# Corner sums through PSUM slots, an inverse transform moved into another loop, and new due times for a hand-made instruction order

## The chip, the core and the metric

The kernel runs on one core of a Trainium2 chip. The metric is device time in microseconds (us) of one execution over the whole batch of four samples. An engine is called by its short name: PE is the matmul engine (PEld its weight loads), DVE the vector engine, ACT the scalar engine, POOL the GpSimd engine and SP the engine that issues plain DMAs.

## What is computed

The input is x of shape (4, 96, 128, 128). Four layers follow one another, each as x + layer(groupnorm(x)):

```python
x = x + L0(gn(x))   # 1x1 projection and 3x3 depthwise conv, a selective scan over 16384 pixels in both directions, 1x1 projection
x = x + L1(gn(x))   # 3x3 conv of 32 channels, fractional and plain Fourier mixing of 64, then a 3x3 conv of all 96
x = x + L2(gn(x))   # deformable 3x3 conv
x = x + L3(gn(x))   # mask, 2-D cosine transform, four state-space scans on quadrants, inverse cosine transform
```

Layer 2 is where the change begins. Small convolutions give for each output pixel and each of nine taps an offset and a mask; the tap's sample is a bilinear mix of four corners, times the mask, and the nine samples of 96 channels go through one weight matrix each:

```python
for k in range(9):
    py, px = base_y + i + dy[k], base_x + j + dx[k]
    samp = ((1-wy)*(1-wx)*v00 + (1-wy)*wx*v01 + wy*(1-wx)*v10 + wy*wx*v11) * mask[k]
    out += einsum('bchw,oc->bohw', samp, weight[:, :, i, j])
```

## The kernel before, in words

**Two lanes and a scan.** The samples are pipelined. `front` (layers 0 and 1, and the offsets of layer 2) of sample b+1 is lane 1; `back` of sample b (layer 2's gather, the head of layer 3, and its forward cosine transform) is lane 0. Both are issued together, and after them `layer3` runs the scans of sample b alone. The inverse transform of sample b-1 (`inverse`) stands at the head of lane 1. So the execution is: front of sample 0 alone; M0 (back 0, front 1) and a scan stage; M1 (back 1, inverse 0, front 2) and a scan stage; M2 (back 2, inverse 1, front 3) and a scan stage; M3 (back 3, inverse 2) and a scan stage; the last inverse alone. M0 to M3 are names that this text uses for the merged stages.

**How the order is made.** Nothing in a lane goes to the engines directly. `Program.record` (line 296) keeps each operation with its data dependencies and an estimated cost (`Program.cost`, line 351). `Program.issue` (line 372) then plays the stage through: it takes the operation that can start soonest, and among those of its engine that could start within `LATENCY` = 0.2 us of that moment the one with the smallest key. The order so found is the program order of each engine; the engines then run it at their own pace, each in order, and wait on semaphores. An operation's key is its due time: each lane is first played alone (`measure`), and the key is the start found there, divided by the last start of its lane, so that both lanes go from 0 to 1 together. Before the change, inverse and front are measured one after the other as one lane; where a stage has no inverse, its front begins at the inverse's end in that list. A scalar-engine operation that needs another function table is taken to start 1.3 us later. `weigh`, `turn` and `finish` are recorded at fixed places of the gather's loop, but their place in the queues comes from this planner.

**The gather (`gather`, line 1270).** For each of 128 image rows, nine indirect DMAs on POOL (one a tap) fetch, for 128 pixels, the four corners of 96 channels each from a table in DRAM into `l_g`, a tile of 128 partitions x 9 taps x 384 numbers; three rows can be held. `weigh` (line 1297) makes the sums of corners in two halves, five taps and four. In each half, ACT multiplies corner 0 of every tap by its weight (one number a partition) into `l_acc`, a PSUM tile of 5 x 96 numbers, of which there is one; DVE then adds corner 1 of every tap onto it in place, then corner 2 in place, and then corner 3 into the SBUF tile `l_sm`. `turn` transposes `l_sm` on PE and ACT copies the transposes to `l_sT` (one copy for the first half, two for the second). `finish` multiplies four rows at a time with the weights, and DVE adds bias and the residual.

**Layer 0 (`layer0`, line 601).** Statistics of the input; then pool `l0a`, the convolution: per group of 512 pixels nine matmuls and one for the gate, two silus on ACT, two stores; then pool `l0b`, the scan: 64 pieces of 512 pixels, each with a softplus in several ACT operations, DVE products and a DVE scan. Its PSUM pool has five banks under the tags a (2), b (1) and c (2); c is used in the scan alone.

**The inverse (`inverse`, line 1461).** 24 pieces of four channels: load, four matmuls (`t_p`), copy by ACT (`t_t`), four matmuls, DVE adds the residual, store; in PSUM banks of its own, two for each of the two products.

Of the kernel before, what the change touches and what calls it, by code (L numbers as in the profile page):

```python
# [9 lines left out]

# [226 lines left out]
class Program:  # L237
# [6 lines left out]
    SPAN = (1.0, 1.0)  # L244
    ENGINES = {"tensor": "PE", "vector": "DVE", "scalar": "ACT", "gpsimd": "POOL", "sync": "SP"}
    TABLES = {AF.Silu: 1, AF.Exp: 2, AF.Ln: 2, AF.Sqrt: 3, AF.Sigmoid: 4, AF.Sin: 5}

    def __init__(self, tc, engines):
# [4 lines left out]
        self.count, self.starts = [0, 0], ([], [])  # L253
# [22 lines left out]
    def measure(self, lane, steps):  # L276
        self.trial, self.lane = True, lane
        tried = []
        self.tried = tried
        run(steps)  # L280
        self.issue(lane)
        at = self.starts[lane]
        t0 = at[-1] + 1e-3 if at else 0.0
        at += [t0 + op.start for op in tried]
        self.end()
        self.trial = False

    def end(self):
        self.issue(0)
        self.issue(1)  # L290
        for pool in self.kept:
            pool.close()
        self.kept, self.count = [], [0, 0]
        self.restart()

    def record(self, engine, name, args, kw):
# [6 lines left out]
            key=self.count[self.lane], wait=0, ready=0.0, then=[], done=False, table=None,  # L303
        )
        if self.trial:
            self.tried.append(op)
        else:
            at = self.starts[self.lane]
            op.key = self.SPAN[self.lane] * at[self.count[self.lane]] / at[-1]
        self.count[self.lane] += 1  # L310
# [40 lines left out]
    def cost(self, engine, name, out, ins):  # L351
# [9 lines left out]
        if engine == "ACT":  # L361
            return 0.12 + (0.0009 if name == "copy" else 0.0011) * n, None
# [7 lines left out]
        return (0.1 if n < 200 else 0.14) + n / (1900 if fast else 960), None  # L370

    def issue(self, lane):

        while self.left[lane]:
            starts = []
            for op in self.able:
                start = max(self.free[op.engine], op.ready)
                if op.table and self.table and op.table != self.table:
                    start += 1.3
                starts.append((start, op.key, op.lane, len(starts), op))  # L380
# [5 lines left out]
            self.able.remove(op)  # L386
            engine, name, args, kw = op.call
# [102 lines left out]
NB = H // BR  # L490
# [3 lines left out]
class Net:  # L494
# [99 lines left out]
    def front(self, xin, T):  # L594

        T.x1, T.x2 = self.plane("x1"), self.plane("x2")
        yield from self.layer0(xin, T)
# [3 lines left out]
    def layer0(self, xin, T):  # L601
# [3 lines left out]
        with self.program.pool(name="l0w", bufs=1) as wp, self.program.pool(name="l0p", bufs=1, space=PSUM) as ps:  # L605
# [44 lines left out]
            with self.program.pool(name="l0a", bufs=3) as wa:  # L650
# [24 lines left out]
                yield from staggered((block(i) for i in range(NB)), 16)  # L675

            with self.program.pool(name="l0b", bufs=3) as wb:
# [96 lines left out]
    def layer1(self, T):  # L774
        nc, a = self.nc, self.a
        mix_d = [self.plane(f"mix{i}", (4, 32, L)) for i in range(2)]
# [493 lines left out]
    def gather(self, T, wp, wb, ps):  # L1270
# [25 lines left out]

        def weigh(row, m):
# [4 lines left out]
            acc = ps.tile([128, 5, C], F32, name="l2_acc", tag="acc", bufs=1)  # L1302
            w4 = work[row // 4].w4
            taps = range(5 * m, 5 + 4 * m)
            for q in range(4):
                for k in taps:
                    at = 36 * (row % 4) + 4 * k + q
                    g, w = gts[row][:, k, q * C : (q + 1) * C], w4[:, at : at + 1]
                    a_ = acc[:, k - 5 * m, :]
                    if q == 0:  # L1310
                        nc.scalar.activation(a_, g, AF.Copy, scale=w)
                    else:
                        o = sms[row][:, k, :] if q == 3 else a_
                        nc.vector.scalar_tensor_tensor(o, g, w, a_, ALU.mult, ALU.add)
# [103 lines left out]
    def transform2(self, src, mat, ps, wt, tags, extra, done):  # L1418
# [4 lines left out]
        def piece(cb):  # L1423
# [7 lines left out]
            p1 = ps.tile([128, 4, 128], F32, name="t2_p1", tag=tags[2])  # L1431
# [6 lines left out]
            p2 = ps.tile([128, 4, 128], F32, name="t2_p2", tag=tags[3])  # L1438
# [22 lines left out]
    def inverse(self, T, out):  # L1461

        nc = self.nc
        if self.program.trial:
            T.yd_d, T.x3 = self.plane("yd_d"), self.plane("x3")
# [727 lines left out]
```

## Time and profile before

| what | us |
|---|---|
| median of 3 runs (18076.4 to 18091.04) | 18077.28 |
| the profiled execution, its own time | 18104.76 |
| span of the profiled execution, first to last instruction | 18103.0 |
| busy in the span: PE / DVE / ACT / POOL | 14334.4 / 13403.8 / 9535.0 / 10677.0 |
| gathers on POOL, 4608, mean of one | 4498.8, 0.976 |
| DVE products into l_acc, 9216, mean of one | 2964.5, 0.322 |
| DVE products into l_sm, 4608, mean of one | 1141.3, 0.308 |
| ACT products into l_acc, 4608, mean of one | 1582.8, 0.344 |

A profile page of this kernel gives all operations the same line, 65, since a recorder issues them; groups are told apart by tile names, output before the arrow and inputs after it. Where the busy time of a group is below its count times the mean, its instructions overlap one another. The page's busy shares are means over stages with different limits, so the reading goes by stretches of time. The boundaries of the stages are seen from the tiles that belong to each: the first front runs from 0 to 1621 us, M0 to 4073, M1 from 5812 to 8340, M2 from 10077 to 12607, M3 from 14345 to 16290, the last inverse from 18028 to the end, with the scan stages between.

### The profile page before, as it was taken

Reading aid. Unit: us, or ns where it says so; the run is one execution under the profiler, and the core shown is the slowest. Engines: PE = TensorE matmul, PEld = TensorE weight load, DVE = VectorE, ACT = ScalarE, POOL = GpSimd, SP = SyncE. Lnnn points to the kernel's source line nnn. Section 1 sums busy time; section 2 is a strip of 40 time slices with the busy share of each in tenths; the row PEclk is TensorE's granted clock in tenths of the full one; section 3 lists DMA queues with packets and bytes.
Section 4 is the critical chain, followed back from the end, with each engine's and each line's share of the span. In section 5 each row is a group of like instructions: output and inputs, shape, how many; then the busy total and the mean of one; then the engine's idle time right before and its main releaser. Section 6 shows DMA issues by size and latency. Waiting matters only on the chain. (4 is left out here: it accounts for less than half of the span.)

```text
span 18103.0 us, 171591 instructions
## 1 busy us (share of the span) xinstructions
PE 14334.4 (79%) x41152; PEld 6500.9 (36%) x41152; DVE 13403.8 (74%) x26226; ACT 9535.0 (53%) x20127; POOL 10677.0 (59%) x9556
## 2 busy tenths in 40 slices
PE   7896887988898787898999687798899722248898
PEld 2263323543333332634333332454333311123334
DVE  1625696678998587577999678566999766668997
ACT  1612463337776364335777356334777522227776
POOL 0102664527888565443888666451888766647887
PEclk9998887999999887898999788798999855579999
DMA  3525666550001657553000556665000254440001
GB/s 81 161 78 168 180 175 201 172 182 14 8 8 51 190 173 207 155 177 99 8 8 8 158 175 180 186 185 163 6 9 8 84 148 142 142 125 13 8 7 49
DMA packets 1189539, 1940.84 MB, mean 107 GB/s; under 512 B 191984, under 2 KB 711600, under 8 KB 1169456
## 3 DMA queue, kind: packets, MB, share of 16 engines
q1 hardware_dynamic: 893616, 1023.60, 19.4%
q0 software_dynamic: 294912, 906.26, 17.1%
q8 instruction: 329, 5.39, 0.1%
q14 instruction: 682, 5.59, 0.1%
HBM read 1473.67 MB, written 455.61 MB: 107 GB/s over the span
## 5 line engine op out<-in xcount | busy, mean ns | idle before, releaser
L65 POOL DMA_INDIRECT l_g<-quad_d,l_i x4608 | 4498.8, 976 | 4204.9 <-ACT l_acc L65 1827.8
L65 POOL TENSOR_TENSOR l_hc<-l_h,l_cs 128x512 f32<-128x512 f32 x3072 | 3854.1, 1274 | 846.6 <-PE l_py L65 267.5
L65 DVE SCALAR_TENSOR_TENSOR l_acc<-l_g,l_v,l_acc 128x96 f32<-128x96 f32 x9216 | 2964.5, 322 | 1816.8 <-ACT l_acc L65 1540.5
L65 DVE TENSOR_TENSOR_SCAN l_h<-l_dA,l_carry,l_dB 128x512 f32<-128x512 f32 x3072 | 3916.3, 1275 | 166.0 <-ACT l_carry L65 72.9
L65 ACT ACTIVATE l_acc<-l_g,l_v 128x96 f32<-128x96 f32 x4608 | 1582.8, 344 | 3396.8 <-DVE l_sm L65 2755.2
L65 ACT ACTIVATE l_dA<-l_dl,l_al 128x512 f32<-128x512 f32 x3072 | 2182.7, 722 | 803.4 <-DVE l_h L65 802.7
L65 PE MATMUL l_pt<-ident,l_sm 128*128 128x128 f32 (+1 forms) x3584 | 843.5, 343 | 2037.8 <-DVE l_sm L65 1954.8
L65 PE MATMUL l_py<-l_hc,ident 128*128 128x512 f32 x4608 | 2385.9, 607 | 20.2 <-POOL l_hc L65 12.1
L65 DVE TENSOR_TENSOR l_dB<-l_du,l_pB 128x512 f32<-128x512 f32 x3072 | 2135.1, 695 | 319.1 <-POOL l_du L65 28.1
L65 PE MATMUL l_pB<-l_bc,pick 128*128 128x512 f32 x3072 | 1769.3, 576 | 567.1 <-DVE l_dB L65 535.3
L65 ACT COPY l_cs<-l_pC 128x512 f32<-128x512 f32 x3072 | 1783.0, 580 | 629.6 <-PE l_pC L65 533.5
L65 PE MATMUL l_pC<-l_bc,pick 128*128 128x512 f32 x3072 | 1543.7, 503 | 112.5 <-ACT l_cs L65 102.1
L65 PEld LDWEIGHTS l_pt<-ident,l_sm 128*128 128x128 f32 (+1 forms) x3584 | 536.5, 157 | 2774.3 <-issue 2096.9
L65 PEld LDWEIGHTS l_pB<-l_bc,pick 128*128 128x128 f32 x3072 | 580.8, 189 | 2228.5 <-DVE l_dB L65 2132.1
L65 DVE SCALAR_TENSOR_TENSOR l_sm<-l_g,l_v,l_acc 128x96 f32<-128x96 f32 x4608 | 1141.3, 308 | 132.0 <-PE l_pt L65 88.7
L65 PE MATMUL l_pu<-l_xq,l_wc 96*64 96x512 f32 (+1 forms) x2048 | 1074.4, 614 | 13.6 <-ACT l_xq L65 13.6
L65 PE MATMUL l_pc<-rows,l_wc 96*96 96x508 f32 (+2 forms) x2304 | 1065.8, 605 | 14.0 <-DVE rows L65 14.0
L65 PE MATMUL l_p<-rows,l_c 96*96 96x508 f32 (+2 forms) x2304 | 1044.2, 597 | 24.6 <-DMA rows<-cat_d 21.8
L65 PEld LDWEIGHTS l_py<-l_hc,ident 128*128 128x128 f32 x4608 | 877.2, 192 | 379.5 <-issue 174.3
L65 POOL TENSOR_TENSOR l_hc<-l_hc 128x512 f32<-128x512 f32 x768 | 977.6, 1273 | 55.2
L65 PE MATMUL l_pc<-l_sT,l_wk 128*96 128x512 f32 (+1 forms) x1792 | 1002.9, 676 | 1.2 <-ACT l_sT L65 1.2
L65 PEld LDWEIGHTS l_pC<-l_bc,pick 128*128 128x128 f32 x3072 | 582.7, 190 | 995.5 <-ACT l_cs L65 670.6
(252 smaller groups left out, 20676.5 us busy)
## 6 DMA issues: line engine op xcount, KB each, us to landing
quad_d<-l_qt SPq DMA_DIRECT2D x124, 768.0 KB
x<-l_x SPq DMA_DIRECT2D x384, 192.0 KB
l_g<-quad_d,l_i POOLq DMA_INDIRECT x4608, 3.4
mix<-l_mx SPq DMA_DIRECT2D x256, 256.0 KB
sp_in<-mix SPq DMA_DIRECT2D x256, 256.0 KB
l_uc<-u_d SPq DMA_DIRECT2D x256, 192.0 KB
l_x<-x SPq DMA_DIRECT2D x256, 192.0 KB
l_xs<-x SPq DMA_DIRECT2D x116, 256.0 KB
```

The source lines that it names most:

```text
L65: ins = op(*args, **kw).ins
```

## The change

Three things are changed, and the planner's numbers with them. First, `weigh` makes two ACT products a tap (corners 0 and 2) into slots of one PSUM tile of five slots that is kept for the whole gather and used in turn; DVE adds corner 1 onto the first and corner 3 onto the second, writing to SBUF (`l_sm` and a new tile `l_part`), and one DVE addition a half row joins the two. Second, `inverse` no longer stands ahead of the front but is handed to `layer0`, where it is taken in turn with the blocks of the convolution; its matmuls use layer 0's two PSUM banks of tag c, which then serve both products. Where there is no front (M3 and the end), it runs alone as before, on two banks instead of four. Third, due times are kept by plan (front, back, both, inverse) and each plan is divided by its own last start; during layer 0's scan the due times advance at a tenth of the pace, from there to the beginning of layer 1. The costs of short ACT and DVE operations are raised, and a table switch now costs its 1.3 us only in the time that is played, while in the choice it adds 0.006 to the key.

```diff
     SPAN = (1.0, 1.0)
+    SWITCH = 0.006
...
+    def go(self, lane, plan):
+        self.lane, self.at, self.count = lane, {**self.at, lane: self.starts[plan]}, 0
+
+    def measure(self, lane, plan, steps):
+        self.trial, self.lane, self.tried, self.count = True, lane, [], 0
         run(steps)
-        self.issue(lane)
-        at = self.starts[lane]
-        t0 = at[-1] + 1e-3 if at else 0.0
-        at += [t0 + op.start for op in tried]
         self.end()
-        self.trial = False
+        now = before = 0.0
+        for op in sorted(self.tried, key=lambda op: op.start):
+            now += op.pace * (op.start - before)
+            op.due, before = now, op.start
+        self.starts[plan] = [op.due for op in self.tried]
+        self.trial, self.pace = False, 1.0
...
-            return 0.12 + (0.0009 if name == "copy" else 0.0011) * n, None
+            return (0.12 if n > 200 else 0.25) + (0.0009 if name == "copy" else 0.0011) * n, None
...
-        return (0.1 if n < 200 else 0.14) + n / (1900 if fast else 960), None
+        return (0.125 if n < 200 else 0.14) + n / (1900 if fast else 960), None
+
+    def switches(self, op):
+        return bool(op.table and self.table and op.table != self.table)
...
-                if op.table and self.table and op.table != self.table:
-                    start += 1.3
-                starts.append((start, op.key, op.lane, len(starts), op))
+                late = self.SWITCH * self.switches(op)
+                starts.append((start, op.key + late, op.lane, len(starts), op))
...
+            if self.switches(op):
+                start += 1.3
...
-            with self.program.pool(name="l0a", bufs=3) as wa:
+            with self.program.pool(name="l0a", bufs=3) as wa, self.program.pool("l3i", 2) as wt:
...
-                yield from staggered((block(i) for i in range(NB)), 16)
-
+                jobs = [staggered((block(i) for i in range(NB)), 16)]
+                yield from staggered(jobs + ([beside(ps, wt)] if beside else []), 1)
+
+
+            self.program.pace = 0.1
             with self.program.pool(name="l0b", bufs=3) as wb:
...
     def layer1(self, T):
         nc, a = self.nc, self.a
+        self.program.pace = 1.0
...
+        acc = ps.tile([128, 5, C], F32, name="l2_acc", tag="acc", bufs=1)
+        turns = itertools.count()
+
         def weigh(row, m):
...
-            acc = ps.tile([128, 5, C], F32, name="l2_acc", tag="acc", bufs=1)
-            w4 = work[row // 4].w4
-            taps = range(5 * m, 5 + 4 * m)
-            for q in range(4):
-                for k in taps:
-                    at = 36 * (row % 4) + 4 * k + q
-                    g, w = gts[row][:, k, q * C : (q + 1) * C], w4[:, at : at + 1]
-                    a_ = acc[:, k - 5 * m, :]
-                    if q == 0:
-                        nc.scalar.activation(a_, g, AF.Copy, scale=w)
-                    else:
-                        o = sms[row][:, k, :] if q == 3 else a_
-                        nc.vector.scalar_tensor_tensor(o, g, w, a_, ALU.mult, ALU.add)
+            taps = slice(5 * m, 5 + 4 * m)
+            part = wb.tile([128, 5, C], F32, name="l2_part", tag="part")
+            sm = sms[row][:, taps]
+            g4 = gts[row][:, taps].rearrange("p k (q c) -> p k q c", c=C)
+            for k in range(5 - m):
+                at = 36 * (row % 4) + 4 * (5 * m + k)
+                w = [work[row // 4].w4[:, at + q : at + q + 1] for q in range(4)]
+                for q, out in ((0, sm), (2, part)):
+                    slot = acc[:, next(turns) % 5, :]
+                    nc.scalar.activation(slot, g4[:, k, q, :], AF.Copy, scale=w[q])
+                    nc.vector.scalar_tensor_tensor(
+                        out[:, k, :], g4[:, k, q + 1, :], w[q + 1], slot, ALU.mult, ALU.add
+                    )
+            nc.vector.tensor_tensor(sm, sm, part[:, : 5 - m], ALU.add)
...
-            p1 = ps.tile([128, 4, 128], F32, name="t2_p1", tag=tags[2])
+            p1 = ps.tile([128, 4, 128], F32, name="t2_p1", tag=tags[2], bufs=2)
...
-            p2 = ps.tile([128, 4, 128], F32, name="t2_p2", tag=tags[3])
+            p2 = ps.tile([128, 4, 128], F32, name="t2_p2", tag=tags[3], bufs=2)
...
-            tags = ("in", 4), ("mid", 2), "a", "b"
-            yield from self.transform2(T.yd_d, dct, ps, wt, tags, take, put_out)
+        tags = ("in", 4), ("mid", 2), "c", "c"
+        yield from self.transform2(T.yd_d, dct, ps, wt, tags, take, put_out)
+
+    def inverse_alone(self, T, out):
+        with self.program.pool("l3ip", 2, PSUM) as ps, self.program.pool("l3i", 2) as wt:
+            yield from self.inverse(T, out, ps, wt)
...
+        if b + 1 == n and b > 0 or b == n:
+            program.go(1, "inverse")
+            run(net.inverse_alone(samples[b - 1], o_all[b - 1]))
+        elif b > 0:
+            program.go(1, "both")
+            run(net.front(x_all[b + 1], samples[b + 1], inverse(samples[b - 1], o_all[b - 1])))
+        elif b + 1 < n:
+            program.go(1, "front")
             run(net.front(x_all[b + 1], samples[b + 1]))
```

## The prediction

> **What bounds the kernel now.** I read the busy shares by stretch first, with stretches cut where the stages begin and end. Columns: stretch, length, busy us (count) of PE, PEld, DVE, ACT, POOL, granted clock, DMA share, GB/s.
>
> ```profile
> 0.00:1621.00 1621.00, 1367.92 (x4314) 659.80 (x4314) 651.58 (x1120) 527.87 (x1103) 83.63 (x68) 0.95 0.40 114
> 1621.00:4073.00 2452.00, 2007.84 (x6176) 944.61 (x6176) 1763.87 (x4796) 1073.53 (x2737) 1263.03 (x1248) 0.87 0.62 183
> 4073.00:5812.00 1739.00, 1536.45 (x3728) 622.62 (x3728) 1553.47 (x1736) 1294.06 (x2272) 1418.50 (x1140) 0.97 0.03 9
> 5812.00:8340.00 2528.00, 2045.23 (x6560) 1000.98 (x6560) 1781.46 (x4820) 1090.34 (x2761) 1261.98 (x1248) 0.87 0.63 186
> 14345.00:16290.00 1945.00, 674.20 (x2246) 361.69 (x2246) 1195.33 (x3707) 565.47 (x1653) 1134.55 (x1184) 0.62 0.51 148
> ```
>
> In order: front of sample 0 alone; M0 (back of sample 0 beside front of 1); a layer-3 scan stage, which four times makes 6952 us and is not edited; M1 (M2 is its twin at 2530); M3 (back of 3 beside the third inverse). No engine fills M0 to M3, so their phases come next: convolution, layer-0 scan and layer 1 alone in the first front, then the same three in M1.
>
> ```profile
> 118.00:397.00 279.00, 275.04 (x640) 105.22 (x640) 12.03 (x11) 42.04 (x65) 0.00 (x0) 1.00 0.27 74
> 397.00:746.00 349.00, 316.50 (x704) 111.82 (x704) 301.38 (x384) 295.43 (x546) 83.43 (x64) 0.97 0.43 127
> 746.00:1427.00 681.00, 626.66 (x2368) 363.49 (x2368) 179.98 (x325) 109.12 (x285) 0.00 (x0) 0.93 0.38 110
> ...
> 6057.00:6395.00 338.00, 321.72 (x850) 130.84 (x850) 183.31 (x581) 119.46 (x307) 177.72 (x183) 0.97 0.58 171
> 6395.00:6992.00 597.00, 477.34 (x1040) 173.54 (x1040) 536.11 (x1237) 410.78 (x927) 381.84 (x344) 0.85 0.60 174
> 6992.00:8028.00 1036.00, 864.01 (x3007) 460.31 (x3007) 674.80 (x2029) 349.61 (x1024) 517.62 (x540) 0.87 0.62 182
> ```
>
> The same stretches for the gather's tile alone count 183, 280 and 540 gathers, at nine a row: 20, 31 and 60 rows. The scan is bound by DVE (536 of 597); a row costs it (597-349)/31 = 8.0 us. The convolution is bound by PE (322 of 338).
>
> What bounds the gather itself is seen in M3, where it is nearly alone (timeline: start, length, instructions merged, idle time before and who ended it):
>
> ```profile
> 15003.72 0.72 ACT L65 ACTIVATE l_acc<-l_g,l_v 128x96 f32<-128x96 f32 x2 [4.86 <-DMA l_g<-quad_d,l_i]
> 15004.38 0.47 ACT L65 COPY l_sT<-l_pt 128x384 f32<-128x384 f32 x1
> 15004.75 0.72 ACT L65 ACTIVATE l_acc<-l_g,l_v 128x96 f32<-128x96 f32 x2
> ...
> 15005.50 2.83 DVE L65 SCALAR_TENSOR_TENSOR l_acc<-l_g,l_v,l_acc 128x96 f32<-128x96 f32 x8 [1.81 <-ACT l_acc L65]
> ...
> 15008.36 0.99 DVE L65 SCALAR_TENSOR_TENSOR l_sm<-l_g,l_v,l_acc 128x96 f32<-128x96 f32 x4
> ...
> 15009.39 0.72 ACT L65 ACTIVATE l_acc<-l_g,l_v 128x96 f32<-128x96 f32 x2 [3.92 <-DVE l_sm L65]
> ...
> 15010.09 0.94 POOL L65 DMA_INDIRECT l_g<-quad_d,l_i  x1 [1.86 <-ACT l_acc L65]
> ```
>
> ACT and DVE take turns, one waiting while the other works. DVE's first product needs only the first slot of l_acc, written by 15004.07, yet starts at 15005.50, 0.03 us after the last slot of the half row. Half rows begin at 15003.72, 15009.39 and (five taps) 15016.60: 12.88 us a row, and 200 us stretches of M3 hold some 136.5 gathers, 13.2 us a row with the work of every fourth row. POOL issues each 1.25 us, 11.25 us a row, then waits. So the gather is this serial sum: 9 ACT products at 0.378, 18 DVE at 0.358, 9 at 0.225, four hand-overs of 0.03: 12.0, and about 0.9 for copies caught between products.
>
> [...] the 1.81 us wait above is for slots that the instruction doesn't touch. [...] here l_dl<-l_dl,l_tmp of 96x512 has a median of 681. [...] here the 194 loads take 1283 on average.
>
> **The change, part by part.** All against the profiled execution: span 18103, time 18104.76; the median shown is 27 us lower, which I subtract at the end.
>
> *Corner sums.* A row loses 18 DVE products at 0.358 (6.4 us) and gains 9 at 0.225, the SBUF-out form of l_sm (2.0), and two adds, [...]: DVE is relieved of 3.2 us. ACT gains 9 products of 0.378, 3.4 us. Over a sample that is 410 us off DVE and 435 on to ACT, which was busy 1090 of 2528. The five slots are one PSUM bank, so ACT writing the next slot and DVE reading the last one still exclude each other; the ring doesn't make them overlap. Each ACT product now waits for a DVE read and DVE's for it; behind it on ACT stand the front's silus and PSUM copies, for whose banks PE waits, but the wait is one sum (0.34 us), where before ACT stood up to 4.86 behind half a row. The serial sum is set by the order in the queues. In pairs (two products, two sums): 0.378+0.344+0.034+0.225+0.308+0.035 = 1.32 a tap, 11.9 a row. One by one: 0.344+0.034+0.308+0.035 = 0.72, times 18 is 13.0. Ideal ring: the gather's 11.25. In M3 the plan gets a tap each 1.25 us, so pairs are likely: 11.9 and 0.6 for copies and adds (they now fit better into the other engine's turn) make 12.5, 0.7 less than 13.2, times 128: **-90**. Beside the front, taps are often all there at once, so I take the middle, 12.5, and 1.2 for front work in the way (M0's convolution has 440 us for 32 rows, 13.75, where the sum is 12.0, so 1.7 before): **13.7 a row**.
>
> *Little gather beside the scan.* The order on an engine goes by due times, each divided by the last of its plan. This rule can be tried on before: with 1945 us of back, gather done at 0.90, and an inverse of 75, stats 36, conv 279, scan 349, layer 1 681, offsets 194 us, it says 34 rows by the convolution's end and 65 by the scan's; M1 has 37 and 68. With the scan at a tenth and the inverse inside the convolution (95 us of PE): 44 and 48. What engines leave idle is still filled with gather, so 7 rows in the scan instead of 31, which then takes 349 + 7x8 = 405, say 400.
>
> *Inverse beside the convolution.* Its own 173 us in M1 go; it held 12 rows, which must be done elsewhere. Its 384 matmuls, 24 copies (0.585) and 24 adds (0.683) go into the convolution: 95 us of PE onto the engine that bounds it, 14 of ACT and 16 of DVE, which are free there. Nothing of it runs on POOL. Its 72 DMAs pass on SP's queue between the rows' loads; DMA share was 0.58 there and 0.83 in the inverse, 19 MB more over some 560 us: hidden. Two PSUM banks instead of four: in the last inverse alone (75 us), a slot is held about 1.8 us, two a piece, on two slots 1.8 us a piece under PE's 2.2: nothing, at worst 10.
>
> *M0.* Stats 74 with 5 rows; convolution 440 for 32 rows as before; scan 400; layer 1 with 84 rows by the gather's sum 84x13.7 = 1151 (by PE (627+84x4.4)/0.93 = 1072, a row's PE being 4.4): 2065 against 74+440+595+1031 = 2140. *M1, M2.* Stats 73; convolution with 39 rows: PE (275+95+39x4.3)/0.96 = 560, gather 534; scan 400; layer 1 with 77 rows: gather 1055, PE 1038, some of each late, 1075: 2108 against 173+72+338+597+1036 = 2216. Neither limit is ever met exactly: I give back 20 a stage. So **-55** in M0, **-88** each in M1 and M2. Offsets with head and transform (312 a stage) stay.
>
> *Planner's constants.* New ACT and DVE costs and the table-switch rule only reorder. Bounds: 10 of 18 table loads fall in the 312 us of the offsets; saving all is -13 a stage, six more +8. I take 0, and 0 for the first front and the scans' stages.
>
> *Sum.* -55-88-88-90 = -321: 18103-321 = 17782, less 27: **17760**. In doubt about the row's price by 0.5 us, 348 rows give 175: 17590 to 17940.
>
> **Rivals.** *Slower: the turns get dearer.* Strict alternation has 36 hand-overs a row where there were four, and each may find the other engine inside a 0.6 us instruction of the front: 13.0+2 = 15 a row. Then M0 74+400+116x15 = 2214, +74; M1 and M2, with 15 for the inverse, 2229, +13 each; M3 at 14.0 a row, +100: 18103+200-27 = **18275**. It decides from 14.4 a row in M0, 14.9 in M1, 13.2 in M3. For it: DVE's 1.81 us wait. Against: ACT and DVE have over 60% idle in the convolution. *The slots do overlap:* M3 at POOL's 11.25, -250; merged stages at PE's sum, M0 74+400+(275+627+505)/0.95 = 1955, -185, M1 and M2 with 95 more 2055, -160 each: 18103-755-27 = **17320**. Against: the wait shown. *It comes to nothing:* rows pushed out of the scan cost 13.7 in a chain where they cost 8 of DVE; should the two cancel: 18077.
>
> **How the numbers follow.** Chances: my sum 0.50, dearer turns 0.22, overlap 0.16, nothing 0.12. 0.2% (36 us) is about what a measurement of this kernel tells from no change. Faster is 0.50+0.16 = 0.66, same 0.12, slower 0.22. The range runs from near the overlap case, 17380, to just short of the dearer turns' middle, 18250.
>
> **What would show it.** Right: in M3, pairs of l_acc on ACT and of sums on DVE with waits under 0.5 us and some 12.5 us a row; scans near 400 us with under ten rows; DVE in M1 down by some 400, ACT up by as much. Wrong: POOL never waiting in M3 (overlap), single products in alternation at 14 us a row (dearer turns), scans still near 600, or a gather that runs on into the offsets, leaving head and transform (188 us alone) uncovered.

## The result, and the profile after

The changed kernel takes 17773.96 us (median of 4 runs, 17757.5 to 17779.59) where the kernel before takes 18079.41 beside it: a ratio of 0.983 (0.981 to 0.985). The forecast was 17760. The profiled execution took 17757.5 us, with a span of 17755.7.

The stages first, in the columns of the prediction: stretch, length, busy us (count) of PE, PEld, DVE, ACT, POOL, granted clock, DMA share, GB/s. All operations have line 66 in this kernel. In order: first front, M0, a layer-3 scan stage, M1, M3; then M1 in its phases: statistics; convolution with the inverse in it; layer 0's scan; layer 1; offsets with head and transform.

```profile
0.00:1624.00 1624.00, 1372.00 (x4314) 662.68 (x4314) 652.87 (x1120) 531.71 (x1103) 81.42 (x68) 0.95 0.39 114
1624.00:4050.00 2426.00, 1947.64 (x6176) 923.86 (x6176) 1568.08 (x3900) 1467.01 (x3889) 1273.78 (x1248) 0.88 0.63 184
4050.00:5789.00 1739.00, 1533.65 (x3728) 624.03 (x3728) 1553.65 (x1736) 1293.61 (x2272) 1418.19 (x1140) 0.97 0.03 9
5789.00:8235.00 2446.00, 1983.19 (x6560) 974.43 (x6560) 1576.81 (x3923) 1480.79 (x3913) 1269.86 (x1248) 0.88 0.66 192
14161.00:15936.00 1775.00, 651.72 (x2246) 358.97 (x2246) 950.40 (x2810) 989.85 (x2805) 1161.90 (x1184) 0.65 0.56 162
```

```profile
5789.00:5902.00 113.00, 37.77 (x114) 20.05 (x115) 59.90 (x156) 42.43 (x115) 63.96 (x66) 0.61 0.83 227
5902.00:6378.00 476.00, 402.22 (x1286) 189.31 (x1284) 258.82 (x761) 295.91 (x833) 318.84 (x322) 0.92 0.72 213
6378.00:6755.00 377.00, 343.96 (x809) 124.18 (x809) 327.00 (x489) 326.62 (x658) 132.25 (x109) 0.98 0.51 147
6755.00:7890.00 1135.00, 914.53 (x3173) 480.48 (x3173) 668.34 (x1908) 645.46 (x1905) 685.47 (x696) 0.87 0.67 195
7890.00:8235.00 345.00, 284.71 (x1180) 160.42 (x1179) 262.75 (x612) 170.37 (x404) 69.34 (x57) 0.88 0.62 189
```

What to see: M0 is 26 us shorter, M1 82, M2 83 (2447 from 2530), M3 170. First front and layer-3 stages stand as they were, the last inverse is 82 us instead of 75. In M1 DVE has 205 us less work and ACT 390 more, and M1 won only 82. Beside the scan lie 5.0 rows (45 gathers by the gather's tile) where there were 31, and 2.8 rows have run on into the offsets, which had none before. Here and below the convolution is cut where its gate's first and last activation stand, in every kernel alike; the kernel before then has 168 us of inverse in M1, 415 of statistics and convolution, 595 of scan, 1037 of layer 1 and 313 of offsets.

In M3, the timeline (start, length, instructions merged, idle time before and who ended it) shows what became of the turns:

```profile
15000.61 0.72 ACT L66 ACTIVATE l_acc<-l_g,l_v 128x96 f32<-128x96 f32 x2 [0.61 <-DVE l_part L66]
...
15001.37 0.31 DVE L66 SCALAR_TENSOR_TENSOR l_sm<-l_g,l_v,l_acc 128x96 f32<-128x96 f32 x1 [0.79 <-ACT l_acc L66]
15001.60 0.31 DVE L66 SCALAR_TENSOR_TENSOR l_part<-l_g,l_v,l_acc 128x96 f32<-128x96 f32 x1
15001.94 0.66 DVE L66 TENSOR_TENSOR l_sm<-l_sm,l_part 128x480 f32<-128x480 f32 x1
15001.94 0.72 ACT L66 ACTIVATE l_acc<-l_g,l_v 128x96 f32<-128x96 f32 x2 [0.60 <-DVE l_part L66]
```

Two products, two sums, two products: a tap each 1.33 us (15000.61 to 15001.94), with each engine idle while the other touches the slots (DVE 0.79 us, ACT 0.60). In the whole trace no ACT product into `l_acc` overlaps a DVE instruction that reads it (9216 of each); in that of before none does either (4608 and 13824). DVE's addition, which reads no slot, runs beside ACT's next pair. From the inverse's end to the last sum the stage's remaining 113.9 rows take 1397 us, 12.27 a row; before, 116 rows took 1578, 13.60.

### The profile page after: what moved, and what is told of

The parts are those of the page before. It is cut to its first block, busy times and chain, and to the rows that moved or that the text cites. A ratio compares the mean times of both kernels' runs of the same rounds, so it can differ in the third digit from the quotient of the medians.

```text
span 17755.7 us, 171824 instructions
## 1 busy us (share of the span) xinstructions
PE 14126.8 (80%) x41152; PEld 6431.4 (36%) x41152; DVE 12556.5 (71%) x22642; ACT 11138.5 (63%) x24735; POOL 10731.0 (60%) x9556
## 5 line engine op out<-in xcount | busy, mean ns | idle before, releaser
L66 POOL DMA_INDIRECT l_g<-quad_d,l_i x4608 | 4552.4, 988 | 3454.4 <-issue 1218.2
L66 ACT ACTIVATE l_acc<-l_g,l_v 128x96 f32<-128x96 f32 x9216 | 3170.0, 344 | 2599.8 <-DVE l_part L66 1557.3
L66 DVE SCALAR_TENSOR_TENSOR l_sm<-l_g,l_v,l_acc 128x96 f32<-128x96 f32 x4608 | 1408.1, 312 | 1693.4 <-ACT l_acc L66 1552.0
L66 PE MATMUL l_pt<-ident,l_sm 128*128 128x128 f32 (+1 forms) x3584 | 793.9, 329 | 1829.3 <-ACT l_acc L66 706.6
L66 DVE SCALAR_TENSOR_TENSOR l_part<-l_g,l_v,l_acc 128x96 f32<-128x96 f32 x4608 | 1428.0, 310 | 1021.2 <-ACT l_acc L66 1009.7
L66 POOL TENSOR_TENSOR l_du<-l_du,l_dl 96x512 f32<-96x512 f32 x256 | 329.3, 1287 | 1263.9 <-DVE l_dl L66 841.6
```

The lines of the kernel that those rows point to most:

```text
L66: ins = op(*args, **kw).ins
```

## The experiments

Theory: the gather is paced by ACT and DVE excluding each other in one PSUM bank, and the change wins by making those turns shorter and by taking gather from the scan. Rivals: the moves and the planner's numbers carry the gain and the sums little; or the order of the products, not the bank, makes the turns.

| kernel | us, median | before beside it | ratio (95%) |
|---|---|---|---|
| e1_sbuf_slots | 18489.19 | 18507.86 | 0.999 (0.998 to 1.000) |
| e2_one_slot | 19432.77 | 18507.86 | 1.050 (1.048 to 1.052) |
| e3_old_sums | 18543.02 | 18507.86 | 1.002 (1.001 to 1.003) |
| e4_only_sums | 20582.46 | 18507.86 | 1.113 (1.111 to 1.114) |
| e3b_old_sums | 18003.6 | 18096.41 | 0.995 (0.993 to 0.997) |
| e1b_sbuf_slots | 16991.43 | 18096.41 | 0.939 (0.938 to 0.941) |
| e8_old_switch | 19511.61 | 18096.41 | 1.078 (1.077 to 1.080) |
| e7_old_costs | 18035.53 | 18096.41 | 0.997 (0.996 to 0.998) |
| e9_before_sbuf | 17559.43 | 18089.76 | 0.971 (0.969 to 0.972) |
| e10_two_banks_last | 17665.33 | 18089.76 | 0.976 (0.975 to 0.978) |
| e6_inverse_ahead | 17855.41 | 18089.76 | 0.987 (0.985 to 0.989) |
| e5_pace08 | 17898.84 | 18089.76 | 0.989 (0.988 to 0.991) |

The first four ran together on another chip, on which the kernel before took 18508 us. The waits of ACT in e1_sbuf_slots (tile that waits, what it waited for: us in all, times, longest) show what is different there:

```profile
ACT l_sT L66 <- remote: 1082.5, 137, 21.1
...
ACT l_sT L66 <- issue: 377.1, 210, 14.0
ACT l_acc L66 <- issue: 322.2, 292, 11.6
```

These are waits for which the profile names no instruction of this core. The same kernel run again on another chip (e1b) has 6.0 us of such waits before l_acc and none before l_sT. Its engines' queues hold the same instructions in the same order, but for a few places on DVE, so it is not the plan that differs. The stages without gather are equal on both chips (1740 us). So sizes are taken from the later runs only, on chips where the kernel before takes 18090 to 18096 us (quiet ones, below), and the first four serve where a trace shows a mechanism. What held the engines on that chip stays open.

### The slots in SBUF: e1_sbuf_slots and e1b_sbuf_slots

```diff
-        acc = ps.tile([128, 5, C], F32, name="l2_acc", tag="acc", bufs=1)
+        acc = wb.tile([128, 5, C], F32, name="l2_acc", tag="acc", bufs=1)
```

> The changed kernel with one edit: the tile of five slots lies in SBUF, not in a PSUM bank, so that ACT can write one slot while DVE reads another. Theory (the gather is a serial sum of ACT and DVE turns, because the slots share a PSUM bank): in M3 a row falls from about 12.4 us to between 11.3 and 11.7 us, close to the 9 gathers at 1.25 us that POOL issues; M3 shorter by about 100 us, M0 to M2 by some 40 to 80 each, in all 17,450 to 17,600 us. Rival (the engines' own work, not the exclusion, sets the gather; the gain came from relieving DVE): within 50 us of the changed kernel's 17,774; ACT writing to SBUF may even cost more than 0.344 us a product. A time above 17,774 would say that the write to SBUF is dear.

> The changed kernel with the ring of five slots in SBUF instead of one PSUM bank. The same kernel as e1_sbuf_slots, run again for the same reason. Theory (ACT and DVE exclude each other only because the slots share one PSUM bank): pairs go, ACT writes while DVE reads, M3's row falls from 12.36 us to the gather's 11.25 to 11.5, M3 -100 to -125; merged stages -20 to -60 each; in all 17,480 to 17,610, a ratio to before of 0.967 to 0.974. Rival (the ring itself or the order in the queues sets the turns): M3 stays at 12.4 a row, 17,774, ratio 0.983.

Measured on a quiet chip: 16991.43, a ratio 0.043 below the changed kernel's and far below the theory's range. M1, its convolution and layer 1, and M3:

```profile
5553.00:7785.00 2232.00, 1924.05 (x6560) 963.71 (x6560) 1517.90 (x3924) 1364.76 (x3913) 1290.92 (x1248) 0.90 0.70 210
5646.00:6073.00 427.00, 384.95 (x1294) 183.01 (x1292) 240.92 (x763) 264.68 (x837) 322.45 (x324) 0.95 0.79 238
...
6459.00:7443.00 984.00, 878.35 (x3170) 478.59 (x3170) 635.21 (x1909) 572.97 (x1904) 689.21 (x681) 0.89 0.75 222
13499.00:15167.00 1668.00, 662.36 (x2246) 356.24 (x2246) 969.25 (x2811) 901.92 (x2805) 1154.98 (x1184) 0.64 0.59 172
```

M3 is 107 us shorter than in the changed kernel, with 114.8 rows in 1312 us, 11.43 a row: what the theory said. The order in the queues is no rival here: from M3's first gather on, ACT and DVE have the same instructions in the same order as in the changed kernel. The merged stages, for which the theory said 20 to 60, won 241, 214 and 212. There the edit does more than change the memory. The planner keeps the writes to one PSUM tile in their written order and leaves those to an SBUF tile free, and in M0 to M2 it found another order at 3027 of ACT's 19634 places. How much of the gain is the bank's and how much the order's was not tested. In layer 1 (984 us for 75.7 rows) PE is now busy 878 us and nearest to filling it. PE's waits for copies of the front fell there (for sp_tb from 24.6 us to 14.3, for l_mx from 15.4 to 8.8), which fits a turn that, while it waits, also holds up the front's work behind it; that this is the reason is argued, not shown. On the first chip M3 of this kernel took 1975 us, and the whole kernel showed no gain.

### Two banks instead of one, where there is room: e10_two_banks_last

```diff
-        acc = ps.tile([128, 5, C], F32, name="l2_acc", tag="acc", bufs=1)
+        banks = 2 if getattr(T, "last", False) else 1
+        accs = [ps.tile([128, 5, C], F32, name=f"l2_acc{i}", tag=f"acc{i}", bufs=1) for i in range(banks)]
...
-                    slot = acc[:, next(turns) % 5, :]
+                    at_ = next(turns)
+                    slot = accs[at_ % banks][:, at_ // banks % 5, :]
...
+            samples[b].last = b + 1 == n
```

> The changed kernel with the slots in two PSUM banks, used in turn, in the last sample's gather alone (M3, where two banks are free; elsewhere one bank as it was). Theory (one bank is the limit, not PSUM): ACT's next product and DVE's sum of the last one run at once, M3's row goes from 12.36 us to 11.3 to 11.6, M3 -90 to -125, all else as in the changed kernel: 17,650 to 17,690, ratio 0.976 to 0.979. Rival (any PSUM slot makes them take turns, or the ring's order does): M3 at 12.4 a row, 17,774, ratio 0.983.

Measured: 17665.33, in the theory's range. M3, and its timeline:

```profile
14189.00:15845.00 1656.00, 658.51 (x2246) 356.00 (x2246) 965.08 (x2810) 888.62 (x2805) 1146.82 (x1184) 0.65 0.60 173
```

```profile
15000.80 0.61 ACT L66 ACTIVATE l_acc<-l_g,l_v 128x96 f32<-128x96 f32 x2 [0.63 <-DMA l_g<-quad_d,l_i]
15001.18 0.31 DVE L66 SCALAR_TENSOR_TENSOR l_sm<-l_g,l_v,l_acc 128x96 f32<-128x96 f32 x1 [0.66 <-ACT l_acc L66]
...
15002.07 0.61 ACT L66 ACTIVATE l_acc<-l_g,l_v 128x96 f32<-128x96 f32 x2 [0.25 <-DMA l_g<-quad_d,l_i]
```

DVE starts 0.38 us after the pair does, while ACT's second product still runs, and ACT waits for the gather, no longer for DVE. 114.8 rows in 1304 us are 11.36 a row. The edit also makes ten slots of five, but e1b reaches the same row with five. The queues of ACT and DVE are those of the changed kernel, all but four places on ACT. So in M3 it is the one bank that costs, not PSUM as such and not the order.

The bank costs in two ways, which these runs do not part: ACT and DVE wait for each other, and ACT's second product waits for its own first. In M3 two products start 377 ns apart in one bank and 281 in two. Nine pairs a row, 0.096 us each, make an estimate of 0.86 us from the second way alone, against a gain of 0.91 (12.27 to 11.36); and at POOL's pace (a gather each 1.25 us in this trace too, 11.25 a row) a row has no more to gain.

### The kernel before with its accumulators in SBUF: e9_before_sbuf

```diff
-            acc = ps.tile([128, 5, C], F32, name="l2_acc", tag="acc", bufs=1)
+            acc = wb.tile([128, 5, C], F32, name="l2_acc", tag="acc", bufs=2)
```

> The kernel before, whole, with one edit: its accumulators l_acc lie in SBUF, in two buffers, instead of in one PSUM bank. Theory (the shared bank is what makes ACT and DVE take turns, in the old sums too): DVE's 18 products at about 0.33 and 9 at 0.225 are 8 us a row, so M3 goes to the gather's 11.25 to 11.6 us a row from 13.6, -230 to -270; the scans stay bound by DVE (593); layer 1's 60 rows come nearer to PE's 864/0.87 = 993, -30 to -40 in each merged stage, the rest -20: 17,610 to 17,720, ratio to before 0.973 to 0.980. Rival (the order of the products in the queues makes the turns, and only the new order of the sums can use another memory): M3 within 20 us of 1942, 18,080, ratio 0.998 to 1.002.

Measured: 17559.43, faster than the whole change, by this one line, and 50 us beyond the theory's range. M1, its scan and layer 1, and M3:

```profile
5701.00:8152.00 2451.00, 2050.10 (x6560) 985.83 (x6560) 1780.13 (x4819) 1053.06 (x2761) 1299.12 (x1248) 0.87 0.65 191
6279.00:6884.00 605.00, 475.12 (x1043) 162.94 (x1043) 571.51 (x1243) 403.01 (x926) 397.37 (x349) 0.88 0.60 173
6884.00:7834.00 950.00, 853.69 (x3004) 456.26 (x3004) 645.05 (x2012) 326.68 (x1015) 528.31 (x532) 0.88 0.67 197
14081.00:15743.00 1662.00, 786.84 (x2246) 360.36 (x2246) 1232.54 (x3706) 616.23 (x1653) 1148.29 (x1184) 0.64 0.60 173
```

M3 is 283 us shorter and runs at 11.39 a row (116.4 in 1326), with the old three DVE products a tap. Layer 1 fell from 1037 to 950; the scan, at 605, gained nothing. So it was not DVE's work that made the old sums slow: its busy time in M1 is the same (1780 us). But the line changes three things at once: the memory, one buffer to two, and the order, since the planner may now take the products tap by tap. In M3, where DVE before made up to ten products into l_acc in a row, the trace here (below) has two, then the one into l_sm, and DVE's queue differs at 1394 of 5464 places. The rival of the order is therefore not excluded by this run; for the new sums it is excluded, by e1b and e10 in M3. A single buffer in SBUF, or the old order there, was not run.

```profile
14903.96 0.38 ACT L65 ACTIVATE l_acc<-l_g,l_v 128x96 f32<-128x96 f32 x1 [0.93 <-DMA l_g<-quad_d,l_i]
14904.37 0.67 DVE L65 SCALAR_TENSOR_TENSOR l_acc<-l_g,l_v,l_acc 128x96 f32<-128x96 f32 x2 [0.28 <-ACT l_acc L65]
...
14905.08 0.32 DVE L65 SCALAR_TENSOR_TENSOR l_sm<-l_g,l_v,l_acc 128x96 f32<-128x96 f32 x1
```

### One slot for all products: e2_one_slot

```diff
-                    slot = acc[:, next(turns) % 5, :]
+                    slot = acc[:, 0, :]
```

> The changed kernel with one edit: every product goes to slot 0, so product and sum alternate strictly. Theory (what was gained in M3 is the pairing of turns: 1.32 us a tap in place of 13.0/9 = 1.45): a row in M3 costs 18 x 0.72 = 13.0 us and what comes on top, 13.4 to 13.8 in place of 12.4, so M3 longer by 130 to 180 us, M0 to M2 by 50 to 100 each, in all about 18,100 to 18,250 us (the planner also believes the rows to be slower and may hand the front more). Rival (the ring of five lets both engines overlap): the row would go up by far more than 1.4 us, since all overlap is gone.

Measured on the first chip: 1.050 of the kernel before; 120 rows of M3 took 1856 us, 15.5 a row, and in M1 some 38 rows ran on into the offsets. The trace shows the strict alternation that the prediction's first rival spoke of, one product and one sum each 0.73 us. How much of 15.5 is that chip's cannot be told, since the changed kernel was not run there: the direction is shown, the size is not.

### The old sums in the changed kernel: e3_old_sums and e3b_old_sums

The body of weigh is that of the kernel before, all else is changed.

```diff
-                for q, out in ((0, sm), (2, part)):
...
+            for q in range(4):
+                for k in taps:
...
+                    if q == 0:
+                        nc.scalar.activation(a_, g, AF.Copy, scale=w)
+                    else:
+                        o = sms[row][:, k, :] if q == 3 else a_
+                        nc.vector.scalar_tensor_tensor(o, g, w, a_, ALU.mult, ALU.add)
```

> The changed kernel with the corner sums of before (one ACT product and three DVE products a tap in place in PSUM), so schedule, inverse, costs and pace are the new ones. Theory: M3 goes back to 1945 us (+170), scans stay short (near 370 to 400 us, few rows in them), and the 120 rows outside the scans cost 0 to 1 us more each: 0 to +60 in each of M0 to M2; in all 17,950 to 18,100 us. Rival (in M0 to M2 the sums bring everything and the new order nothing): M0 to M2 as in the kernel of before or slower, 18,077 us or more.

> The changed kernel with the corner sums of the kernel before (inverse beside the convolution, little gather beside the scan and the new planner constants stay). The same kernel as e3_old_sums, run again because that run stood on a chip where ACT, DVE and PE stood over 1000 us in waits for nothing that the profile shows, and where the kernel before took 18508 us instead of 18079. Theory (the sums carry half of the gain): M3 back to 1942 us, +170 against the changed kernel, layer 1 of the merged stages at the old sums' 13.7 us in M3 and about 15.5 beside the front, some +60 to +80 a stage: 18,120 to 18,180, a ratio to before of 1.002 to 1.006 where the chip is quiet. Rival (the moves carry the merged stages, the sums M3 alone): 17,774+170 = 17,944, ratio 0.9925.

Measured on a quiet chip: 18003.6, between theory and rival. Against the changed kernel M3 is 143 us longer (1918), M1 45 (2491), M2 40, M0 8. So of the 0.017 that the change wins, 0.012 is lost without the new sums, most of it in M3; beside the front they are worth little as long as both forms take turns in one bank.

### The new sums in the kernel before, and the old switch rule: e4_only_sums and e8_old_switch

e4 is the kernel before with the new weigh and its ring, and nothing else of the change. Its expectation:

> The kernel of before with the new corner sums alone; order, inverse, costs and pace are the old ones. Theory: M3 shorter by about 170 us; in M0 to M2 the scans still hold some 30 rows, where DVE is relieved of 3.2 us a row and ACT burdened with 3.4, so each scan goes from 597 to some 560 to 600 us, and the merged stages gain 0 to 40 us each; in all 17,790 to 17,910 us. Rival (sums give nothing in merged stages because ACT becomes the scan's bound): scans of 600 us or more, M0 to M2 unchanged or longer, 17,900 us or more.

It ran at 1.113 of the kernel before, far above the theory's range. In its trace M0's convolution begins only when all 128 rows have been gathered: the last gather is issued at 3535 us, the gate's first activation stands at 3561. The next run asks whether the planner's rule does that:

```diff
-                late = self.SWITCH * self.switches(op)
-                starts.append((start, op.key + late, op.lane, len(starts), op))
+                start += 1.3 * self.switches(op)
+                starts.append((start, op.key, op.lane, len(starts), op))
...
-            if self.switches(op):
-                start += 1.3
```

> The changed kernel with the kernel before's rule for ACT operations that need another table: 1.3 us are added to their start before the choice, instead of 0.006 to their due time. Theory (starvation: with the new sums ACT nearly always has a ready product, so an operation that must load a table is never the soonest, and the square root of layer 1's group norm stands behind all 2304 products in the written order, where the changed kernel has it behind 761): each merged stage becomes 478 us of convolution, 377 of scan, the rest of the gather alone (some 83 rows at 12.4 = 1030), then layer 1 alone (706) and the offsets alone (245), with 113 of stats some 2950 in place of 2446: 17,774+3x500 = 19,270, 19,100 to 19,450, ratio 1.057 to 1.076. Rival (planner constants only reorder, as the prediction had it): 17,774 within 60, ratio 0.980 to 0.987.

Measured: 19511.61, just above the theory's range, 1.10 of the changed kernel. Layer 1 of M1 in five cuts, of which the second and the last, and what PE waited for in it:

```profile
7866.00:8166.00 300.00, 89.19 (x269) 43.89 (x268) 162.05 (x517) 180.69 (x528) 220.09 (x228) 0.62 0.55 160
...
8766.00:9224.00 458.00, 450.53 (x1740) 270.13 (x1740) 113.97 (x192) 56.73 (x170) 5.17 (x4) 0.99 0.27 78
```

```profile
PE l_pt L66 <- ACT l_acc L66: 382.3, 74, 6.5
```

The first 934 us of layer 1 hold all its gathers but one (694) and hardly anything of the front, PE 0.3 busy; then layer 1 runs alone. In the written order the square root of its group norm, which loads a table (1.28 us in M1 of the changed kernel), stands behind all 2304 products of the sample; in the changed kernel it stands behind 833 (761 in M0). With 18 products a row instead of 9 ACT nearly always has one that can start within the 1.3 us, so under the old rule the operation that must load is never the soonest. In the written order of e4, too, this root stands behind all 2304 products, and M0's convolution in e8 begins as late as in e4 (last gather at 3174 us, first gate at 3201). That e4 falls to the same rule is thus likely; e4 with the new rule was not run, so what the sums alone are worth stays open.

### The old costs: e7_old_costs

```diff
-            return (0.12 if n > 200 else 0.25) + (0.0009 if name == "copy" else 0.0011) * n, None
+            return 0.12 + (0.0009 if name == "copy" else 0.0011) * n, None
...
-        return (0.125 if n < 200 else 0.14) + n / (1900 if fast else 960), None
+        return (0.1 if n < 200 else 0.14) + n / (1900 if fast else 960), None
```

> The changed kernel with the kernel before's planner costs for short ACT and DVE operations (0.12 instead of 0.25 us ahead of the size term on ACT, 0.100 instead of 0.125 on DVE). Theory (the costs only reorder; the switch rule is the constant that matters): 17,774 within 60, ratio 0.980 to 0.987. Rival (the plan needs true durations to give the front its turns on ACT): over 18,000, ratio above 0.996.

Measured: 18035.53, the rival's case, 0.014 above the changed kernel: M0 42 us longer, M1 99, M2 91, M3 36. M1's layer 1 takes 1212 us for 76 rows instead of 1135 for 77. Layer 1 here, and PE's wait for the Fourier stage's copies in it, first in the changed kernel and then here:

```profile
6808.00:8020.00 1212.00, 960.06 (x3167) 506.60 (x3167) 663.37 (x1888) 642.75 (x1886) 676.59 (x686) 0.83 0.62 181
```

```profile
PE sp_b L66 <- ACT sp_tb L66: 24.6, 26, 2.1
```

```profile
PE sp_b L66 <- ACT sp_tb L66: 41.1, 30, 2.5
```

ACT has the same 18 table loads in M1. Its runs of only one or two products between other work there are 61 instead of 117, and PE stands 41.1 us for the Fourier stage's copies (sp_tb) instead of 24.6: the front's turns on ACT come later. That this is the whole of it is argued, not shown; M3, with no front, is slower too (12.57 a row).

### The inverse ahead of the front: e6_inverse_ahead

```diff
+    def ahead(S, out, xin, T):
+        yield from net.inverse_alone(S, out)
+        yield from net.front(xin, T)
...
-        (1, "both", net.front(x_all[0], T, inverse(T, o_all[0]))),
+        (1, "both", ahead(T, o_all[0], x_all[0], T)),
...
-            run(net.front(x_all[b + 1], samples[b + 1], inverse(samples[b - 1], o_all[b - 1])))
+            run(ahead(samples[b - 1], o_all[b - 1], x_all[b + 1], samples[b + 1]))
```

> The changed kernel with the inverse transform back ahead of the front in M1 and M2 (four PSUM banks, as before), the rest as changed. Theory (the inverse alone is time lost, beside the convolution it costs its 95 us of PE and little else): 182 us of inverse with 14 rows (as M3 shows), then M0's stage less 14 rows, 2425 less 14 times 3 to 6 us, some 2360: 2545 against 2446, +100 in M1 and in M2 each: 17,774+200 = 17,975, 17,930 to 18,020, ratio 0.992 to 0.997. Rival (its rows are gathered there at nearly the gather's own pace, so what it hid before comes back elsewhere): +10 to +30 each, 17,800 to 17,830, ratio 0.985 to 0.987.

Measured: 17855.41, in neither range: 0.004 above the changed kernel, M1 38 us longer and M2 47. The inverse here runs on two PSUM banks, as `inverse_alone` has it after the change, and not on the four that the expectation names; at 159 us for its 12 rows it is no longer than before (168). M1's inverse, and its convolution:

```profile
5799.00:5958.00 159.00, 97.92 (x475) 80.91 (x476) 77.42 (x223) 82.51 (x230) 103.67 (x108) 0.74 0.89 262
6067.00:6461.00 394.00, 342.92 (x912) 140.24 (x910) 194.94 (x578) 232.75 (x648) 247.99 (x250) 0.92 0.62 179
```

Its 108 gathers are 12 rows in 159 us, 13.2 a row: the inverse alone is a stretch in which the gather goes at nearly its own pace. The convolution without it takes 394 us for 27.7 rows, with it 476 for 35.8. So the move is worth some 40 us a stage, and not the inverse's length.

### More gather beside the scan: e5_pace08

```diff
-            self.program.pace = 0.1
+            self.program.pace = 0.8
```

> The changed kernel with the pace beside layer 0's scan at 0.8 instead of 0.1: by the written order some 29 rows lie beside the scan (5 before), 64 beside layer 1 (77) and 31 before the convolution's end (37). Theory (a row costs beside the scan what it cost before, (593-349)/31 = 7.9 us, beside layer 1 (1135-681)/77 = 5.9, beside the convolution some 3): scan 349+29x7.9 = 578, layer 1 1060, convolution 460, offsets 325, with 113 of stats 2536 against 2446, +90 in each merged stage: 17,774+270 = 18,044, 17,950 to 18,090, ratio 0.993 to 1.001. Rival (the new sums take 3.2 us a row off DVE, so a row beside the scan costs (377-349)/5.2 = 5.4 or less, and nothing is won by keeping it away): within 40 us a stage, 17,774 to 17,890, ratio 0.983 to 0.990.

Measured: 17898.84, between the two ranges. The scan and layer 1 of M1:

```profile
6323.00:6932.00 609.00, 489.22 (x1050) 181.73 (x1048) 463.83 (x950) 465.28 (x1130) 353.76 (x312) 0.82 0.56 160
6932.00:7999.00 1067.00, 878.94 (x3047) 464.59 (x3047) 598.54 (x1667) 564.91 (x1656) 567.93 (x577) 0.86 0.64 185
```

With 27.4 rows the scan takes 609 us, (609-349)/27.4 = 9.5 a row, though DVE is busy only 464 of them where it was busy 536 before: PE, the busiest, is busy 0.80 of the time, and a row beside the scan costs more, not less. The rival's reason falls. But keeping 22 of these rows away, which takes 232 us off the scan (609 to 377), gives 68 back in layer 1, 60 in the convolution, 24 in the offsets and 11 in the statistics, so that M1 wins 69 and the kernel 0.007.

## Why the forecast was right, point by point

**The total** is 14 us from the forecast by luck. Against its terms M3 won 80 us more, M0 29 less, M1 and M2 6 and 5 less, and the stages put at nothing grew by 14: 26 more won in all. And 27 us were taken off at the end because the profiled execution before lay above the median; the one after lies 16 below it.

**The bound** is shown for M3: with two banks (e10) or with SBUF (e1b) the row falls to 11.36 and 11.43 us, next to the 11.25 of POOL's issues, with ACT and DVE in the same order. The rival of overlapping slots, 17320, is what was to come had the slots not shared a bank; e1b went 330 beyond it.

**Corner sums.** Pairs at 1.32 a tap were forecast and 1.33 came; ACT's load in M1 came too, 390 us of 435. DVE's relief did not: 205 us where 410 was put, and "down by some 400" among the signs of being right. The sum took each old product at its distance to the next start, 0.358 us, of which DVE is busy 0.323, and each new one at 0.225, where the two of a tap take 0.54. The relief of 3.2 us a row was my estimate in its last part: the trace of before has no addition of the size of a row's two, and its addition of 96x512 (l_dl) has a median of 681 ns. The two took 659 and 558 ns on average, 1.22 us a row, and 1.2 is what the estimate leaves for them, so the miss is not theirs. The waits within a pair, 0.61 us on ACT and 0.79 on DVE, are not under 0.5 either; they are what one engine's turn lasts. The row in M3 was put at 12.5 and is 12.27. The term -90 was mis-sized all the same, -170 measured: I took the old row from 200 us stretches (13.2), where the whole stage, its tail after the last gather included, has 13.60.

**The phases of M1**, and of M0 beside it:

| us | M1 before | forecast | after | M0 forecast | after |
|---|---|---|---|---|---|
| inverse alone | 168 | 0 | 0 | | |
| statistics and convolution | 415 | 633 | 589 | 514 | 529 |
| scan | 595 | 400 | 377 | 400 | 378 |
| layer 1 | 1037 | 1075 | 1135 | 1151 | 1171 |
| offsets, head, transform | 313 | 312 | 345 | 312 | 348 |
| given back for limits not met | | 20 | | 20 | |
| sum | 2528 | 2440 | 2446 | 2397 | 2426 |

M1's forecast is close because its misses cancel. The scan holds 5 rows and not 7; convolution and statistics were 44 us better than PE's sum. That sum put a row at 4.3 us of PE there, where its own lines have (322-275)/20 = 2.4, and PE is busy 440 us in statistics and convolution together, where the sum has 538 for the convolution alone. It also divided PE's busy time by the granted clock, as if this gave a least time; it does not, for layer 1 of e9 would then take 854/0.88 = 970 us, and it takes 950. Layer 1 was 60 us worse: 77.2 rows in 1135 us are 14.7 a row, where I had 13.7 by the gather and 1038 by PE, and met neither. And 2.8 rows spilled into the offsets, which take 33 us more, a step that I had at no change; a gather that runs on into them was among the signs of being wrong. In M0 the row in layer 1 is 14.6, just beyond the 14.4 from which the dearer turns decide, and M0 wins 26 and not 55.

**Costed at nothing.** Besides the offsets, four steps. The planner's constants, "only reorder", 0: this step failed. Without the new switch rule the kernel is at 1.078, without the new costs at 0.997. The forecast's row assumed an order in which the front gets its turns on ACT, and without these constants the order is another. I had counted table loads (10 of 18 in the offsets, 1.28 us each on average), and in M1 their number is 18 with the old costs and the old rule too; what changed is what stands ahead of them. First front (+3) and layer-3 stages (+4 for all four) held. The last inverse, 0 to 10, is +7.

**The scan is bound by DVE**: that this is what a row costs there was not shown. In e5, M1's scan has 72 us less DVE work than in the kernel before and fewer rows, and is no shorter (609 us against 597).

**The inverse.** 173 us were to go, with 12 rows coming back and 95 us of PE entering the convolution; that balance was of the right kind, and e6 gives its net, some 40 us a stage. Taken back one at a time from the changed kernel, the move of the inverse costs 76 us in all, the pace 119, the sums 217 and the planner's costs 255, each taken from the ratios by 18080. They are not parts of one sum: taking back the switch rule alone puts the kernel some 1400 above the kernel before.

## What to carry to other kernels

When two engines take turns over different slots, ask first whether the slots share a PSUM bank: here one line that moves a tile to SBUF was worth 0.029 in the old kernel (with a second buffer and another order) and 0.043 in the new one (with another order in M0 to M2), against 0.017 for the whole rewrite. Where an order is planned from costs, twice as many short operations on an engine can starve whatever the plan holds back by a fixed penalty; look where rare operations stand in the written order. Price a moved piece of work by what the stage grows by, not by its busy time: a row cost 9.5 us beside the scan and the inverse alone hid 12 rows at 13.2.

## What the runs showed of the hardware

Two ACT products that follow one another into one bank start 377 ns apart (median in M3, changed kernel); into two banks, or into SBUF, 281. In the trace the second of a pair in one bank waits on ACT's own semaphore for the first and starts 33 ns after its end, so this part of the price is in how the instructions are made to wait. The turns between ACT and DVE, too, are waits on semaphores that the instructions carry (a sum starts 33 ns after the last product's end, the next product 35 ns after the last sum's: medians in M3, changed kernel); in the traces of before and after the two are never in that bank at once, so what would happen if they were is not shown. The mean product takes 344 ns into PSUM (changed kernel) and 367 into SBUF (e1b), and yet the kernel with the slower one is 0.043 faster.

Also unexpected: one chip was slower with the same programs. On it the kernel before took 2.4% longer, the old sums in the changed kernel 3.0% (18543 against 18004) and the slots in SBUF 8.8% (18489 against 16991), with waits that the profile ascribes to nothing. In the traces of the last two the extra time lies in the stages with gather alone.
